# First adjacency chunks, first weight's queues, sum order and code rows of the second layer, last norm's order

## The chip, the cores and the metric

The kernel runs on one core of a Trainium2 chip. The metric is the device time of one execution in microseconds (us); the profile's span, from the first to the last instruction, is 1.8 us shorter.

## The reference, cut to what matters

Two graph layers on x (4096 x 512 float32) and adj (4096 x 4096 int32, about 32 ones in a row).

```python
# layer 0: at most the first 64 neighbours of a row
keep = (adj > 0) & (cumsum(adj > 0, axis=1) <= 64)
cnt  = keep.sum(axis=1)
xj   = leaky_relu((keep @ x / max(cnt, 1)) @ W_nb.T + b_nb)
xi   = leaky_relu(x @ W_line.T + b_line)
x1   = layernorm(x + xi + where(cnt > 0, xj, 0))
# layer 1: dense attention
wh   = x1 @ W + bW
e    = leaky_relu((wh @ a1 + b1)[:, None] + (wh @ a2 + b2)[None, :], 0.2)
out  = layernorm(x1 + softmax(where(adj > 0, e, -9e15)) @ wh)
```

## The kernel before

Rows are taken in 32 blocks of 128; "x i" below is block i of x, 256 KB, loaded by four DMAs of 64 KB. Five stages follow each other on TensorE (PE).

**Head (L362).** `load_squares` (L287) splits 128 rows of x, or a quarter of a weight, into four DMAs over a tuple of queues (SP, ACT, POOL); `turn_squares` transposes what has landed on VectorE (DVE). `by_quarters` multiplies x 0 with W_nb quarter by quarter, then x 1 with the whole of W_nb, then both with W_line. `spin` keeps PE busy until then. All DMAs of SP and ACT count their landings on eight semaphores in turn, those of POOL on eight others; each DMA waits, in its queue, for the earlier one on its semaphore. So at most eight of either kind are under way.

**y stage (`seven`, L493).** Blocks go in pairs g = 1 to 15, and each pair takes seven products in this order: x_g with w11, x_p with t3 (p is the pair before), bank_z with t1, bank_w with w22, x_g with t2, x_p with t4, bank_y with w21. One step lasts 12.04 us on PE. `turn_pair` (L294) transposes the next two blocks on DVE and has POOL load two more (x tiles rotate over three buffers); L557 is the DVE sum that must have read x_p before the product with t4 writes there. Between the products, `steps` puts work in from lists of four: in steps 1 and 2 the DVE sums `fold_w(c)` (L379, folding W with a1 and a2), from step 3 on the codes of adj. A chunk of adj (1 MB, `load_adj`, L157, SP, two buffers) goes through `edge` on ScalarE (ACT, L168), scans on DVE and `pack`. `fold_end` writes the folded `wa` to DRAM (`wa_d`, L386, SP, 1024 single words).

**Aggregation (L738).** 32 blocks, 14.5 us each.

**wh stage (L1202, L889).** wh = x1 W. Steps j count 128 permuted rows; `seven_wh` takes a pair g in two parts. `turn_x1` (L821) transposes what `load_turned` (L795, SP) loaded; `first_wh` makes two quarter products, ACT copies one into `bt` (L898) and `sum_wh` (L901, DVE) adds the other into the bank `xv` on which the next products pile up. L939 is the ACT copy of `xv` into its neighbour half, for the product with t1. `sums_x1` (L878, L879) and `sums_x2` (L884, L885) are sums for the next pair. `load_nat` (L948) brings the first two halves of the code rows of block 0 on ACT's queue, four DMAs of 64 KB each; `cover` (L960) reads them first at step 7.

**Attention (L1075) and tail.** 64 parts of 56 products; after the last one the final two blocks are summed and normed on DVE (L1287 to L1290, `ln_rs`, `ln_apply`), with one power on POOL (L126) for each.

The order of instructions on each engine is written out by hand in these loops (`manual_schedule`), and each engine keeps it.

Of the kernel before, what the change touches and what calls it, by code (L numbers as in the profile page):

```python
# [8 lines left out]
F32 = mybir.dt.float32  # L9
# [10 lines left out]
P = 128  # L20
# [11 lines left out]
def two_layer_adj_gnn(  # L32
# [16 lines left out]
    nc = tc.nc  # L49
    N, C = x.shape  # L50
    NB = N // P
    NC = C // P
# [18 lines left out]
    stat = ctx.enter_context(tc.tile_pool(name="stat", bufs=4))  # L71
# [43 lines left out]
    def ln_stats(y):  # L115
        st = stat.tile([P, nc.vector.BN_STATS_DIM], F32, name="st")
        nc.vector.bn_stats(st, y)  # L117
        return ln_rs(st)
# [18 lines left out]
    with ExitStack() as l0:  # L137
# [12 lines left out]
        edge_of = {}  # L150
        seen_of = {}

        def load_adj(s):
            if s < NB * NCH:
                b, h = divmod(s, NCH)
                a = adj_p.tile([P, CH], I32, name="a")
                nc.sync.dma_start(a, adj_blk(b)[:, ts(h, CH)])  # L157
                loaded[s] = a

# [117 lines left out]
        with ExitStack() as la:  # L277
# [8 lines left out]

            def load_squares(dst, src, queues):  # L287
                for n in range(NC):
                    queues[n * len(queues) // NC].dma_start(  # L289
                        dst[ts(n, SQ)], src[:, ts(n, P)].rearrange("(j a) c -> a j c", a=SQ)  # L290
                    )

# [6 lines left out]
            def load_turned_x(i, queues=(nc.gpsimd,)):  # L299

                if i < NB:
                    xrs[i] = late[i % 3].rearrange("p (j c) -> p j c", c=P)
                    load_squares(xrs[i], x_blk(i), queues)
# [32 lines left out]
            def load_part(name, src, part, queues):  # L336
                load_squares(raw[name][:, part], src[P * part.start // NC : P * part.stop // NC, :], queues)

            def load_quarter(name, src, c, queues):
                load_part(name, src, slice(NC * c, NC * c + NC), queues)  # L340
# [35 lines left out]
            def fold_w(c):  # L376
                wn = raw["w"][c] if c < NC else early_rows[2]
                for k in range(2):
                    nc.vector.scalar_tensor_tensor(  # L379
                        early_rows[3], wn, 1.0, early_rows[k], ALU.mult, ALU.mult,  # L380
                        accum_out=wa[:, k, c : c + 1] if c < NC else ca[:, k : k + 1],
                    )
# [35 lines left out]
                    y_lo[i], src, y_hi[i].bitcast(F32), ALU.subtract  # L418
                )

            both = (nc.sync, nc.scalar)
            load_turned_x(0, both)
            load_quarter("nb", w_nb, 0, both)
            load_quarter("nb", w_nb, 1, (nc.gpsimd,))
            load_quarter("nb", w_nb, 2, (nc.sync,))
            load_quarter("nb", w_nb, 3, (nc.scalar,))
            load_turned_x(1, both)
            for h in range(2):
                load_part("line", w_line, slice(2 * NC * h, 2 * NC * (h + 1)), both)
            load_turned_x(2, both)  # L430
            spin(12)

            turn_x(0)
            load_turned_x(3, both)
            nc.sync.dma_start(bias_line, b_line.partition_broadcast(P))
            pys[0] = by_quarters(xts[0], "nb")
            turn_x(1)
            load_turned_x(4)
# [172 lines left out]
            for g in range(1, NT):  # L611
                steps = idle
                q = done[0]
                if g == 1:
                    steps = [
                        lambda: load_adj(0),
                        lambda: None,
                        lambda: nc.scalar.activation(few[:, 5:6], three, AF.Sigmoid),
                        lambda: fold_w(0),
                    ]  # L620
                elif g == 2:
                    steps = [
                        lambda: fold_w(1),
                        lambda: (load_adj(1), fold_w(2)),
                        lambda: None,
                        lambda: fold_w(3),
                    ]
                else:
                    flags = lambda: (load_adj(q + 2), edge(q + 1))
                    codes = (lambda: pack(q - 1)) if g > 3 else (  # L630
                        lambda: (edge(0), fold_w(NC), fold_end())
                    )

                    steps = [
                        flags if g > 4 else codes,
                        lambda: scan_sums(q),
                        codes if g > 4 else flags,
                        lambda: scan_codes(q),
                    ]
                    if g == NT - 1:  # L640
                        load_own_x(NB - 1, nc.gpsimd)
                        scan_first = steps[1]
                        steps[1] = lambda: (scan_first(), load_first_kt())
                    done[0] += 1
                seven(g, False, steps)
# [229 lines left out]
    def sums_x1(g):  # L875
        if PLAIN <= g < NS // 2:
            top, low = x1ts[2 * g], x1ts[2 * g + 1]
            nc.vector.tensor_tensor(sum_x(g, 1), low[:, 0:2], low[:, 2:4], ALU.add)  # L878
            nc.vector.tensor_tensor(low[:, 0:2], top[:, 0:2], low[:, 0:2], ALU.subtract)  # L879
# [20 lines left out]
    def sum_wh(g):  # L900
        nc.vector.tensor_tensor(xvs[g % 2][:, 0], bt[:, g, 2], yrs[g % 2][:, 1], ALU.add)  # L901

    def seven_wh(g, part, extra=lambda: None):

        p = g - 1
        new, old = g < NS // 2, p >= PLAIN
        yr, xv = yrs[g % 2], xvs[g % 2]
        yr_p, xv_p = yrs[p % 2], xvs[p % 2]  # L910
        t1, t2, t4, _ = wsums
        if part == 0:
            if new and g > PLAIN:
                first_wh(g)
            if old:
                product_wh(yr_p[:, 0], x1ts.pop(2 * p)[:, 2:4], w21)
                product_wh(xv_p[:, 1], sum_x(p, 1), t1)
            if g == PLAIN + 1:
                sum_wh(g)
            turn_x1(2 * g + 3)  # L920
            sums_x1(g + 1)
            if new and g > PLAIN + 1:
                sum_wh(g)
            if old:
                nc.scalar.copy(bt[:, p, 0:2], yr_p)
            extra()
        else:
            if old:
                product_wh(xv_p[:, 0], x1ts.pop(2 * p + 1)[:, 2:4], t4)
            if new:  # L930
                product_wh(xv[:, 0], sum_x(g, 2), t2)
                product_wh(yr[:, 1], sum_x(g, 4), w22)
            turn_x1(2 * g + 4)
            sums_x2(g + 1)
            if old:
                nc.scalar.copy(bt[:, p, 2:4], xv_p)
                later.append(p)
            if new:
                nc.scalar.copy(xv[:, 1], xv[:, 0])  # L939
            extra()  # L940

    def load_nat(b, h, queue=nc.sync):

        if b < NB:
            nats[b, h] = ep.tile([P, 2, NS * SQ // 2], BF16, name="nat")
            rows = code_d[b].rearrange("(i a) (n x) -> n a i x", a=SQ, n=4)
            for n in range(4):
                queue.dma_start(nats[b, h][ts(n, SQ)], rows[n][:, ts(h, 2), :])  # L948
# [242 lines left out]
    for j in range(NS):  # L1191
        g, h = divmod(j, 2)
        if g < PLAIN:
            if j == 3:

                first_wh(PLAIN)
                sum_wh(PLAIN)
            bank = ps_acc.tile([P, 2, HC], F32, name="acc")
            (yrs, xvs)[g].append(bank)
            x1t = x1ts.pop(j)  # L1200
            for m in range(NC):
                nc.tensor.matmul(  # L1202
                    bank.rearrange("p h c -> p (h c)"), x1t[:, m, :], ws[:, m, :],
                    start=(m == 0), stop=(m == NC - 1),
                )
            nc.scalar.copy(bt[:, g, 2 * h : 2 * h + 2], bank)
            if j == 2:
                sums_w1()
            turn_x1(j + 3)
            if j == 2:  # L1210
                sums_x1(PLAIN)
                sums_w2()
                sums_x2(PLAIN)
            if h == 1:
                later.append(g)
            if j == 3:
                sums_w3()
        else:
            seven_wh(g, h, lambda: weights_step(j))
        load_turned(j + 7)  # L1220
        if j in (1, 2):
            load_nat(0, j - 1, nc.scalar)
        if j in (5, 7):
            combine_wh()
    seven_wh(NS // 2, 0)
# [59 lines left out]
    nc.vector.bn_stats(st[:, 1], low[:, 1])  # L1285
    for h in range(2):
        stt(top[:, h], p[2 + h], rz[:, 0:1], top[:, h], ALU.mult, ALU.add)  # L1287
    top_stats = ln_stats(top.rearrange("p h c -> p (h c)"))
    stt(low[:, 0], p[4], less_rz, low[:, 0], ALU.mult, ALU.add)
    nc.vector.bn_stats(st[:, 0], low[:, 0])  # L1290
    low_stats = ln_rs(st)
    ln_apply(top.rearrange("p h c -> p (h c)"), top_stats)
# [38 lines left out]
```

## Time and profile before

| what | us |
|---|---|
| three runs | 1552.64, 1552.98, 1554.51 (median 1552.98) |
| the profiled execution | 1552.42, its span 1550.6 |
| PE busy | 1538.0 (99%) |
| DVE, ACT, POOL busy | 1267.5, 984.2, 263.1 |
| PE before the first product (L362) | 6.36, with idle products from 1.21 |
| y stage starts, aggregation starts | 21.8, 204.09 |
| wh stage starts, attention starts | 668.44, 769.59 |
| record of the attention's last product ends | 1543.29 |

A line of the timeline has start, duration, engine, source line, operation, out<-in, shapes and, in brackets, how long the engine stood idle before and what released it. The windows have the busy time of each engine in each stretch, the granted clock, the mean busy share of the 16 DMA engines (DMA) and GB/s. A float32 product is two records on PE. Records of one run overlap, since their ends are modelled; so the pace is read from the distance of their starts (0.43 us for 128x512, 0.216 us for 128x256).

### The profile page before, as it was taken

The numbers are of one execution on the slowest core, as the hardware profiler recorded it, in microseconds if no ns is written. First come the engines' busy times: TensorE is split into PE (matmuls) and PEld (weight loads), VectorE is DVE, ScalarE is ACT, GpSimd is POOL, SyncE is SP. The second block draws the span as 40 slices with busy tenths as digits, with TensorE's granted clock in tenths as the row PEclk, the third lists the DMA queues.
The fourth block names the chain that finished last, engine by engine and source line by source line (L and its number), as shares of the span: only waits on it lengthen the run. The fifth ranks groups of instructions, "written<-read, shape, count | busy, mean of one in ns | idle before, by whom it ended". The sixth has DMA issues, their size and how long they took to land.

```text
span 1550.6 us, 19180 instructions
## 1 busy us (share of the span) xinstructions
PE 1538.0 (99%) x6580; PEld 1240.4 (80%) x6580; DVE 1267.5 (82%) x2348; ACT 984.2 (63%) x1186; POOL 263.1 (17%) x422
## 2 busy tenths in 40 slices
PE   9999999999999999999999999999999999999998
PEld 5444478888888888868888888888888888888887
DVE  6888769999999999378887888888888888888864
ACT  2666678888888887427684567555675556755520
POOL 4545322212221212110001101111011110111101
PEclk9999999999999999999999999999999999999999
DMA  9965598888998887654122112221122211222202
GB/s 238 206 207 185 193 254 263 226 269 264 250 260 256 234 263 189 153 126 113 42 61 56 46 36 69 63 60 48 35 69 64 59 49 34 69 66 57 51 5 55
DMA packets 180098, 203.28 MB, mean 131 GB/s; under 512 B 102416, under 2 KB 141072, under 8 KB 171680
## 3 DMA queue, kind: packets, MB, share of 16 engines
q1 hardware_dynamic: 149424, 131.25, 29.5%
q0 software_dynamic: 26416, 68.43, 17.4%
q10 hardware_dynamic: 4160, 2.38, 0.6%
q8 instruction: 51, 0.84, 0.2%
q14 instruction: 47, 0.39, 0.1%
HBM read 142.08 MB, written 43.13 MB: 119 GB/s over the span
## 4 chain that ended last, share of the span: by engine, by line
PE 96%; DMA 2%; DVE 1%; issue 0%; ACT 0%; POOL 0%; SPq 0%; ACTq 0%; DVEq 0%; POOLq 0%
PE acc L1075 36%; PE acc L738 28%; PE pt L1075 14%; PE acc L493 11%; PE acc L889 4%; PE pt L738 2%; PE acc L362 1%; DMA c<-in_x_dram 1%; DMA nat<-code_d 0%; DMA w<-x_d 0%; DMA a<-in_L_gnn_W_nb_dram 0%; DVE c L821 0%; DVE a L821 0%; POOL c L289 0%; DVE st L117 0%
## 5 line engine op out<-in xcount | busy, mean ns | idle before, releaser
L1075 PE MATMUL acc<-bt,s 128*128 128x256 f32 x1504 | 335.7, 379 | 0.0
L1075 PEld LDWEIGHTS acc<-bt,s 128*128 128x128 f32 x1504 | 285.8, 190 | 38.9
L738 PE MATMUL acc<-y_hi,kt 128*128 128x512 f32 x780 | 303.4, 389 | 0.0
L738 PE MATMUL acc<-y_lo,kt 128*128 128x512 f32 x780 | 303.4, 389 | 0.0
L960 ACT ACTIVATE w<-nat,few 128x1024 f32<-128x1024 uint8 x128 | 137.0, 1137 | 237.4 <-DVE a L1035 237.4
L1075 PE MATMUL acc<-bt,a 128*128 128x256 f32 x1056 | 239.0, 379 | 0.0
L1075 PE MATMUL pt<-bt,a 128*128 128x256 f32 x992 | 224.5, 379 | 0.0
L1075 PEld LDWEIGHTS acc<-bt,a 128*128 128x128 f32 x1056 | 200.6, 190 | 27.3
L1075 PEld LDWEIGHTS pt<-bt,a 128*128 128x128 f32 x992 | 188.5, 190 | 25.6
L1035 DVE STREAM_TRANSPOSE a<-w 128x1024 f32<-128x1024 f32 x128 | 153.1, 1225 | 61.8 <-ACT w L1016 51.0
L271 ACT ACTIVATE kt<-ktb,few 128x1024 fp32r<-128x1024 uint8 x124 | 142.6, 1151 | 86.5 <-PE acc L738 68.9
L126 POOL TENSOR_TENSOR rs<-ve,few 128x1 f32<-128x1 f32 x64 | 42.7, 666 | 810.3 <-DVE ve L124 797.0
L738 PEld LDWEIGHTS acc<-y_hi,kt 128*128 128x128 f32 x780 | 146.5, 188 | 30.4
L738 PEld LDWEIGHTS acc<-y_lo,kt 128*128 128x128 f32 x780 | 146.5, 188 | 30.3
L953 ACT ACTIVATE w<-w,st_n 128x1024 f32<-128x1024 f32 x128 | 149.3, 1233 | 16.4 <-DVE m L970 16.4
L1016 ACT ACTIVATE w<-w,nm 128x1024 f32<-128x1024 f32 x128 | 145.5, 1137 | 11.1 <-DVE nm L1007 11.1
L970 DVE CUSTOM_DVE_ANT_0 w<-e_n,w 128x1024 f32<-128x1024 f32 x128 | 149.5, 1220 | 1.3
L168 ACT ACTIVATE edge<-a,few 128x2048 bf16<-128x2048 int32 x64 | 136.3, 2129 | 1.8 <-DVE left L187 1.7
L216 ACT CAST code<-left 128x2048 uint8<-128x2048 bf16 x64 | 121.1, 1893 | 0.0
L199 DVE TENSOR_TENSOR left<-edge,left 128x2048 bf16<-128x2048 bf16 x64 | 78.4, 1225 | 2.2
L187 DVE TENSOR_TENSOR_SCAN left<-few,ends,left 128x1024 bf16<-128x1024 f32 x32 | 75.2, 2351 | 1.1
L187 DVE TENSOR_TENSOR_SCAN left<-few,left 128x1024 bf16<-128x1024 f32 x32 | 73.3, 2291 | 1.1
(230 smaller groups left out, 2041.9 us busy)
## 6 DMA issues: line engine op xcount, KB each, us to landing
a<-in_adj_dram SPq DMA_DIRECT2D x64, 1024.0 KB, 5.8
code_d<-code POOLq DMA_DIRECT2D x64, 256.0 KB, 3.9
nat<-code_d SPq DMA_DIRECT2D x248, 64.0 KB, 2.2
w<-x_d SPq DMA_DIRECT2D x128, 64.0 KB, 2.1
own<-in_x_dram SPq DMA_DIRECT2D x31, 256.0 KB, 3.1
own<-own_d POOLq DMA_DIRECT2D x31, 256.0 KB, 5.1
x_d<-own POOLq DMA_DIRECT2D x31, 256.0 KB, 4.8
out_dram<-c POOLq DMA_DIRECT2D x30, 256.0 KB, 2.7
```

Of the source, the lines that this page charges most:

```text
L168: nc.scalar.activation(edge_of[s], loaded.pop(s).rearrange("p (t q) -> p q t", q=2), AF.Sigmoid, bias=steep[:, 0:1], scale=STEEP, accum_ou ...
L187: nc.vector.tensor_tensor_scan(left[:, 1], three.to_broadcast([P, CH // 2]), left[:, 0], NEIGHBORS + 3.0 if h == 0 else end, ALU.max, ALU. ...
L216: nc.scalar.copy(code.bitcast(U8).rearrange("p (t q) -> p q t", q=2), seen_of.pop(s))
L271: nc.scalar.activation(kts[s], bytes_.rearrange("p t (i r) -> p t r i", r=2), AF.Sigmoid, bias=steep[:, 1:2], scale=STEEP,)
L493: nc.tensor.matmul(bank, lhs[:, k, :], rhs[:, k, :], start=start and k == 0, stop=k == 1, skip_group_check=True,)
L738: nc.tensor.matmul(accs[i], kt[:, k // 2, k % 2, :], term[j], start=(g == n == 0 and term is y_hi), stop=(g == NS - 1 and n == KB - 1 and ...
L953: nc.scalar.activation(dst, src, AF.Prelu, bias=bias, scale=scale, alpha=0.2)
L960: nc.scalar.activation(wts[b][:, i, :], nats[b, i // 2].bitcast(U8)[:, i % 2, :], AF.Relu, bias=far, scale=-FAR,)
L970: nc.vector.tensor_tensor_reduce(w_i, e2_n, w_i, 1.0, -3e38, ALU.subtract, ALU.max, m4s[b][:, i : i + 1])
L1016: nc.scalar.activation(w_i, w_i, AF.Exp, bias=nms[b][:, i : i + 1], accum_out=z4s[g][:, r, i : i + 1])
L1035: nc.vector.transpose(a[:, r].rearrange("p s (i a) -> p i s a", a=SQ), wts[2 * g + r][:, :, ts(k, 8 * SQ)].rearrange("p i (s x) -> p i s x ...
L1075: nc.tensor.matmul(banks[g][n], lhs[:, j, :], bt[:, 4 * k + j, rhs, :], start=(k == 0 and j == 0 and n == mate[0]), stop=(k == NP - 1 and ...
```

## The change

1. **Adj chunks 0 and 1** are no longer asked for in steps 1 and 2 as they are; each load now follows a one-column memset on DVE that stands behind `fold_w(1)` and `fold_w(3)`, and so waits for them.
2. **Head:** `load_squares` deals its four DMAs out in turn. The quarters of W_nb go over SP, ACT and POOL (5, 5 and 6 DMAs, before 6, 6 and 4), x 1, x 2 and x 3 partly over POOL, and b_line is asked for before x 2 and x 3.
3. **wh stage:** `sum_wh` stands ahead of `sums_x1` on DVE. The eight DMAs of the first code rows are issued after step 3 instead of after steps 1 and 2; in ACT's order they now stand between the copy of step 3 (L1206) and the first copy L939.
4. **Tail:** the sum of the lower block's first half stands ahead of the upper block's aggregation (L122) and the wait for its power.

The products on PE keep their order and number; DVE has two memsets more.

```diff
-        def load_adj(s):
+        def load_adj(s, behind=None):
...
                 a = adj_p.tile([P, CH], I32, name="a")
+                if behind is not None:
+                    behind.memset(a[:, 0:1].bitcast(F32), 0.0)
                 nc.sync.dma_start(a, adj_blk(b)[:, ts(h, CH)])
...
-                    queues[n * len(queues) // NC].dma_start(
+                    queues[n % len(queues)].dma_start(
...
-            both = (nc.sync, nc.scalar)
-            load_turned_x(0, both)
-            load_quarter("nb", w_nb, 0, both)
-            load_quarter("nb", w_nb, 1, (nc.gpsimd,))
-            load_quarter("nb", w_nb, 2, (nc.sync,))
-            load_quarter("nb", w_nb, 3, (nc.scalar,))
-            load_turned_x(1, both)
+            sp, act, pool = nc.sync, nc.scalar, nc.gpsimd
+            load_turned_x(0, (sp, act))
+            load_quarter("nb", w_nb, 0, (sp, act, pool, pool))
+            load_quarter("nb", w_nb, 1, (sp, act, pool, pool))
+            load_quarter("nb", w_nb, 2, (sp, act, pool, sp))
+            load_quarter("nb", w_nb, 3, (act, sp, pool, act))
+            load_turned_x(1, (sp, act, pool, pool))
             for h in range(2):
-                load_part("line", w_line, slice(2 * NC * h, 2 * NC * (h + 1)), both)
-            load_turned_x(2, both)
+                load_part("line", w_line, slice(2 * NC * h, 2 * NC * (h + 1)), (sp, act))
+            nc.sync.dma_start(bias_line, b_line.partition_broadcast(P))
+            load_turned_x(2, (act, pool))
             spin(12)
 
             turn_x(0)
-            load_turned_x(3, both)
-            nc.sync.dma_start(bias_line, b_line.partition_broadcast(P))
+            load_turned_x(3, (sp, pool))
...
                 if g == 1:
                     steps = [
-                        lambda: load_adj(0),
+                        lambda: None,
                         lambda: None,
...
                 elif g == 2:
                     steps = [
-                        lambda: fold_w(1),
-                        lambda: (load_adj(1), fold_w(2)),
+                        lambda: (fold_w(1), load_adj(0, nc.vector)),
+                        lambda: fold_w(2),
                         lambda: None,
-                        lambda: fold_w(3),
+                        lambda: (fold_w(3), load_adj(1, nc.vector)),
                     ]
...
             turn_x1(2 * g + 3)
-            sums_x1(g + 1)
             if new and g > PLAIN + 1:
                 sum_wh(g)
+            sums_x1(g + 1)
...
-        if j in (1, 2):
-            load_nat(0, j - 1, nc.scalar)
+        if j in (3, 4):
+            load_nat(0, j - 3, nc.scalar)
...
-    top_stats = ln_stats(top.rearrange("p h c -> p (h c)"))
+    top_st = stat.tile([P, nc.vector.BN_STATS_DIM], F32, name="st")
+    nc.vector.bn_stats(top_st, top.rearrange("p h c -> p (h c)"))
     stt(low[:, 0], p[4], less_rz, low[:, 0], ALU.mult, ALU.add)
+    top_stats = ln_rs(top_st)
     nc.vector.bn_stats(st[:, 0], low[:, 0])
```

## Prediction

> **What bounds the kernel now.** The page first, whose two lines say what there is to win:
>
> ```profile
> PE 1538.0 (99%) x6580; PEld 1240.4 (80%) x6580; DVE 1267.5 (82%) x2348; ACT 984.2 (63%) x1186; POOL 263.1 (17%) x422
> PE 96%; DMA 2%; DVE 1%; issue 0%; ACT 0%; POOL 0%; SPq 0%; ACTq 0%; DVEq 0%; POOLq 0%
> ```
>
> PE is busy but for 12.6 us of the 1550.6, and the change takes no product away. So a gain can only come from PE's holes and from the tail. Where PE waits says the view of its waits (us in total, times, longest):
>
> ```profile
> PE acc L493 <- DVE t L557: 1.6, 1, 1.6
> PE acc L889 <- DVE acc L901: 1.6, 2, 1.1
> PE acc L362 <- DVE wt_nb L294: 0.8, 1, 0.8
> ```
>
> Each of the three is touched by one part. Idle times understate them, as a record's end is modelled; I measure from start to start. The y stage, chain of waits first, then PE's timeline:
>
> ```profile
> 28.12 1.65 POOL c L289 x3
> 29.77 7.78 DMA c<-in_x_dram
> 38.31 0.66 DVE t L557
> ```
> ```profile
> 35.54 1.88 PE L493 MATMUL acc<-hi,lo 128*128 128x512 f32 x4
> 39.01 1.98 PE L493 MATMUL acc<-hi,xt 128*128 128x512 f32 x4 [1.59 <-DVE t L557]
> 40.84 3.60 PE L493 MATMUL acc<-wt_nb,xt 128*128 128x512 f32 x8
> ```
>
> The fourth DMA of x 7 takes 7.78 us from issue to landing; DVE waits for it (3.34 us), then L557, then PE. From 35.54 to 40.84 are 5.30 us for two products that elsewhere take 1.715 each: the hole costs 1.87. Meanwhile SP has both adj chunks under way, issued at 24.0 and 25.4. The windows show the head and a spot to be wary of (columns as in the table's note):
>
> ```profile
> 7.00:8.00 1.00, 0.96 (x9) 0.77 (x7) 0.51 (x1) 0.00 (x0) 0.00 (x0) 1.00 0.55 123
> 8.00:9.00 1.00, 0.72 (x7) 0.53 (x5) 0.29 (x1) 0.00 (x0) 0.00 (x0) 1.00 0.61 179
> 46.00:47.00 1.00, 1.00 (x4) 0.52 (x3) 0.93 (x5) 1.00 (x1) 1.00 (x3) 1.00 0.00 0
> ```
>
> From 7 to 9 the DMA engines are 0.55 and 0.61 busy while PE waits for W_nb: too little is under way, since SP and ACT may not issue. At 46 nothing moves at all, though x 11 has been asked for at 45.83: `wa_d`, issued at 43.74, takes 12.7 us to land (DMA issues), and x 11's four DMAs need 11.2 to 12.1. Last the wh stage, timeline of ACT, DVE and PE:
>
> ```profile
> 680.37 2.23 ACTq L948 DMA_DIRECT2D nat<-code_d  x4
> 685.21 0.36 ACT L939 COPY acc<-acc 128x256 f32<-128x256 f32 x1 [0.33 <-PE acc L889]
> 687.98 0.71 DVE L821 STREAM_TRANSPOSE a<-w 128x512 f32<-128x512 f32 x1 [2.05 <-DMA w<-x_d]
> 690.96 0.42 DVE L901 TENSOR_TENSOR acc<-bt,acc 128x256 f32<-128x256 f32 x1
> ```
> ```profile
> 691.44 1.13 PE L889 MATMUL acc<-s,bt 128*128 128x256 f32 x4 [1.14 <-DVE acc L901]
> 697.83 1.13 PE L889 MATMUL acc<-s,bt 128*128 128x256 f32 x4
> 704.56 1.13 PE L889 MATMUL acc<-s,bt 128*128 128x256 f32 x4 [0.42 <-DVE acc L901]
> ```
>
> DVE gets x1's rows of step 8 2.05 us late, because code rows, x1 rows and broadcasts share the DMA engines; L901 stands behind that, and PE behind L901. By starts, less 0.865 for four records and counting the 0.105 of a restart, the three holes cost 1.42, 0.35 and 0.68.
>
> **Part by part. Head.** No DMA more or less. Quarter 0 now waits for POOL's second DMA; POOL's first four took 2.9 to 3.6 us to land, so it lands near 5.6 instead of 5.4. Quarter 1 (product at 7.56) needs POOL's fourth, as before, so that costs nothing. Quarters 2 and 3 land in turn instead of together, and POOL adds DMAs while SP and ACT wait. If they come just in time, PE goes on from 7.56: four quarters, x 1 next at 10.25 and W_line at 13.7 instead of 14.80, that is 1.1 less. If DMA is the limit after all, 0. I take 1.0, nearer the upper end, as the engines stood 0.84 us idle in those two windows. x 1 comes over three queues as well, so W_line, b_line, x 2 and x 3 are asked for about 1 us sooner. Of POOL's row, what follows is x 4; it is moved past four DMAs at about 0.55 us each, but waits for the transpose of x 1 anyway. The Trainium skill's page "DMA: Bandwidth & Descriptors", section "Issuing engines are not separate DMA queues", speaks against this part: all queues end in the same 16 engines, and spreading saves only issue time. By it this term would be near 0 and the whole 1.0 us smaller; the two windows with idle engines are why I do not follow it here.
>
> **Chunks.** Without 2 MB of adj, what is left in front of x 7 is W, a1, a2 and bW, which also start earlier. x 7 has to land by about 34 instead of 37.55, and its first DMA goes at 28.12 or sooner; even the 5.1 us that POOL's loads of x take at the median is then in time. The hole of 1.87 goes; if something is left of it, at most half. DVE pays two memsets (0.06 each, as that at 10.91), hidden, since DVE stood 3.34 us here. Chunk 0 now leaves at about 33, after `fold_w(1)`; with the 5.8 us of the median chunk, doubled, it lands by 45, and ACT's `edge(0)` (45.49 before, 42.6 after the shift) has some 3 us by the median. Chunk 1 leaves behind `fold_w(3)`, which without DVE's wait ends at about 39.7; `edge(1)` wants it at 47.2. Behind it in SP's queue stands `wa_d`, which so far went with an empty queue. What is late next: x 11, blocked by `wa_d` until 58.96. From its landing to the end of L557 are 1.41 us, and PE's next t4 product, at 63.15 before, comes at 60.3. So x 11 must land by 58.9: no slack is left, each us later costs PE one. Chunk 1 landing at 45.5 puts `wa_d` where it was (its small packets run at 44.5 to 45.7 before), and x 11, asked for at 42.5 to 44 now, may pass ahead. I take 0 for it, with 0 to 2 for the range.
>
> **wh stage.** `sum_wh` moved past two sums of 0.34 to 0.46 pitch is 0.8 earlier; the holes of 0.35 and 0.68 need 0.35 and 0.68. They go: 1.0 us. The two sums are read a pair later. With no code rows at 678 to 688 (8 x 64 KB), x1's rows of step 8 come in time and the 1.42 goes as well. But ACT issues eight DMAs behind the copy at 684.29, and L939 (685.21), L898, L925 and every later copy queue behind them. The first four go at 0.45 each, until 685.7; the next four wait for the landings of the first. PE wants L939's result at 688.41. With landings of 2.0 us the last goes at 687.7, L939 ends at 688.4 and PE loses 0; with the 5.9 of the slowest row it ends at 692.3 and PE loses 3.9; with the median of 2.9, 0.9. DMA is at 0.88 to 1.16 from 680 to 689, lighter by half a MB then; I take 3.6, so a loss of 1.4 against the 1.42 won: 0 (from +1.4 to -2.5).
>
> **Tail.** The sum (L1289) starts when the last product is done, near 1543.3, instead of at 1543.53; aggregation and addition follow it, and the lower statistics start at about 1544.05 instead of 1544.04. Nothing, within 0.15 to either side.
>
> **Sum.** 1.0 + 1.87 + 1.0 + 0 + 0 = 3.9 us off the profiled execution: span 1546.7, time 1548.5. The median of the runs lies 0.56 above that execution, so 1549.1. About 0.2% (3.1 us) is what a measurement of this kernel can tell from no change.
>
> **Rivals.** (1) ACT's queue blocks: PE loses 2.5 us more than I took, and gains stay at 1.4 to 2.5: 1550.5 to 1551.6. For it: ACT issued the last four in 2.23 us, at the landings' pace. Against: step 3 is past the worst of the broadcasts. Chance 0.18. (2) The head does not do what it says, DMA being the limit: 2.9 us, 1550.1. For it, 0.9 busy from 2 to 7 us. Chance 0.12. (3) Slower: chunk 1 lands as slowly as chunks did here (11.7 to 15.4 us), `wa_d` goes behind it and closes the DMA engines for its 12.7 us until 64 to 67 instead of 57; x 11 and chunk 2 stand behind. x 11 at 67 costs PE 8, net 4 slower: 1557. It decides from 62.8 on, 3.9 past 58.9; up to there it only eats the gain. Against it: those chunks ran two at a time beside W, and a late `wa_d` lets x 11 pass. Chance 0.08, and 0.05 for half of it (1551). The forecast itself, all parts about as summed: 0.57.
>
> **Numbers.** The forecast holds 1547.5 to 1549.8, from a head of 1.1 and ACT's block of 0 to a chunk term of 1.5. Of it and some of rival 2 come 0.62 for faster; rivals 1, 2 and half of 3 give 0.30 for the same; 0.08 slower. The range, 1547.5 to 1552.0, reaches over rivals 1, 2 and the half of 3.
>
> **What would show it.** Right: second quarter pair at about 8.5 and W_line's product at 13.7; no PE wait on L557; aggregation at 201.2; L939 of step 5 ending near 689.7 relative to the old clock, and no PE wait on L901. Wrong: the pairs start at 9.5 as before; x 11 landing after 59 with PE waiting on L557 near 60; a PE wait on L939 of over 2 us; the attention starting less than 2 us earlier than at 769.59.

## The result and the profile after

The changed kernel takes 1556.27 us (median of 21 runs, 1553.79 to 1557.91), the kernel before 1553.58 beside it (21 runs, 1551.87 to 1554.90): ratio 1.0018, 95% interval 1.0011 to 1.0025. So it is 2.7 us slower, where the forecast was 1549.1, that is 3.9 faster. The profiled execution took 1556.24, span 1554.5, at its median; the profiled one of before, 1552.42, lay 1.2 under the median of these 21, so the two traces differ by 3.9 us of span where the medians differ by 2.7. Two executions behind the tables below lie far off all others and are left out of the ratios: one of the kernel before (8155.08 us) and the profiled one of a2_no_head (3282.49 us).

The page says that PE is as busy as before. The waits of PE (us in total, times, longest) say that two of the three old ones are gone, that the one for W_nb has grown from 0.8 to 2.0 us, and that a new one, for ACT's copy L941, is longer than any of them:

```profile
PE 1538.9 (99%) x6580; PEld 1241.0 (80%) x6580; DVE 1267.1 (82%) x2350; ACT 983.8 (63%) x1186; POOL 271.0 (17%) x430
```
```profile
PE acc L891 <- ACT acc L941: 3.3, 1, 3.3
PE acc L364 <- DVE wt_nb L296: 2.0, 3, 1.4
...
PE acc L364 <- DVE wt_line L296: 0.5, 1, 0.5
PE acc L495 <- ACT acc L551: 0.5, 1, 0.5
```

(Lines of the changed kernel stand 2 further down: L941 is the L939 of before, L559 its L557, L950 its L948.) Since PE has the same 6580 matmuls in the same order, the two traces can be laid side by side product by product. How late the changed kernel is, at the same product:

| product (its start before) | late by, us |
|---|---|
| first product (6.36) | 0.55 |
| y stage starts (21.81) | 1.35 |
| fourth product of the y stage (26.96) | 2.24 |
| after the hole at L557 (40.84) | 0.38 |
| wh stage, last one before the new wait (687.54) | 0.22 |
| wh stage, after it (688.41) | 3.73 |
| 693.27 | 4.11 |
| 704.56, and from there on | 3.2 |
| last landing of the output | 3.2 |

From the last landing to the end of the span are 2.3 us before and 2.9 after: a closing drain on POOL's queue, which the timeline does not list, takes 5.48 us instead of 4.83 and ends 0.6 later after that landing. The table has the result in three readings. **The head lost 2.2 us** (PE's timeline, first before, then the changed kernel):

```profile
6.36 2.36 PE L362 MATMUL acc<-wt_nb,xt 128*128 128x128 f32 x16
9.48 5.49 PE L362 MATMUL acc<-wt_nb,xt 128*128 128x128 f32 x24 [0.76 <-DVE wt_nb L294]
14.80 7.17 PE L362 MATMUL acc<-wt_line,xt 128*128 128x128 f32 x40
21.81 1.88 PE L493 MATMUL acc<-wt_nb,xt 128*128 128x512 f32 x4
```
```profile
6.91 1.16 PE L364 MATMUL acc<-wt_nb,xt 128*128 128x128 f32 x8 [1.42 <-DVE wt_nb L296]
8.32 2.05 PE L364 MATMUL acc<-wt_nb,xt 128*128 128x128 f32 x16 [0.25 <-DVE wt_nb L296]
10.70 4.76 PE L364 MATMUL acc<-wt_nb,xt 128*128 128x128 f32 x16 [0.33 <-DVE wt_nb L296]
...
17.84 5.49 PE L364 MATMUL acc<-wt_line,xt 128*128 128x128 f32 x24 [0.53 <-DVE wt_line L296]
23.16 1.88 PE L495 MATMUL acc<-wt_nb,xt 128*128 128x512 f32 x4
```

The quarters no longer come two at a time, but the first starts at 6.91 (before 6.36), the second at 8.32 (7.56) and the fourth at 10.70 (10.36); only the third is 0.17 earlier. The last of W_nb landed at 9.74 (before 8.77), the last of W_line at 16.88 (14.99), the last of x 2 and x 3 at 20.32 (18.21). Of the 2.2 us the last 0.9 come in the y stage, before the fourth product, where PE waits for ACT's copy L551 (last line of the waits, 0.5 by the idle time). **The hole before L557's reader is closed**, as forecast; from 37.78 the products follow at 1.72 (same view):

```profile
37.78 1.88 PE L495 MATMUL acc<-hi,lo 128*128 128x512 f32 x4
39.50 1.88 PE L495 MATMUL acc<-hi,xt 128*128 128x512 f32 x4
41.21 3.60 PE L495 MATMUL acc<-wt_nb,xt 128*128 128x512 f32 x8
```

**The wh stage lost 3** (timeline of ACT and PE):

```profile
684.52 7.12 ACTq L950 DMA_DIRECT2D nat<-code_d  x8
...
691.73 0.36 ACT L941 COPY acc<-acc 128x256 f32<-128x256 f32 x1 [6.63 <-DMA nat<-code_d]
...
692.14 1.13 PE L891 MATMUL acc<-s,bt 128*128 128x256 f32 x4 [3.35 <-ACT acc L941]
...
693.11 1.47 PE L891 MATMUL acc<-s,c 128*128 128x256 f32 x4
...
694.37 1.91 PE L891 MATMUL acc<-s,bt 128*128 128x256 f32 x4
...
696.07 1.47 PE L891 MATMUL acc<-w,bt 128*128 128x256 f32 x4
```

The eight issues occupy ACT's queue for 7.12 us: the first four go out by 685.85, and each of the last four waits until one of these has landed, which takes them 4.7 to 5.4 us. The copy behind them starts at 691.73 instead of 685.21, and PE stands 3.35 us. Four matmuls of 128x256 take 0.87 us elsewhere; here the groups at 693.11 and 694.37 take 1.26 and 1.70 from start to start. The windows say why (busy time and count of PE, PEld, DVE, ACT, POOL, then the granted clock, DMA share, GB/s):

```profile
694.00:697.00 3.00, 3.00 (x9) 2.37 (x8) 2.90 (x8) 1.21 (x3) 0.00 (x0) 0.51 0.49 136
697.00:702.00 5.00, 5.00 (x25) 4.41 (x24) 3.22 (x9) 1.85 (x4) 0.00 (x0) 1.00 0.42 118
```

After the wait the granted clock fell to a half for 3.41 us, from 693.55 to 696.97: eight matmuls in 3.39 us instead of 1.73, another 1.7 us lost.

### The profile page after: what moved, and what is told of

It reads as the page before. It is cut to its first block, busy times and chain, and to the rows that moved or that the text cites. A ratio compares the mean times of both kernels' runs of the same rounds, so it can differ in the third digit from the quotient of the medians.

```text
span 1554.5 us, 19179 instructions
## 1 busy us (share of the span) xinstructions
PE 1538.9 (99%) x6580; PEld 1241.0 (80%) x6580; DVE 1267.1 (82%) x2350; ACT 983.8 (63%) x1186; POOL 271.0 (17%) x430
## 4 chain that ended last, share of the span: by engine, by line
PE 97%; DMA 2%; DVE 0%; ACT 0%; issue 0%; ACTq 0%; POOLq 0%; DVEq 0%
PE acc L1077 36%; PE acc L740 28%; PE pt L1077 14%; PE acc L495 11%; PE acc L891 5%; PE pt L740 2%; PE acc L1204 1%; DMA a<-in_L_gnn_W_nb_dram 1%; DMA nat<-code_d 0%; DMA a<-in_L_gnn_W_line_dram 0%; DMA c<-in_x_dram 0%; DVE t L397 0%; DVE hi L502 0%; DVE hi L516 0%; ACTq L291 0%
## 5 line engine op out<-in xcount | busy, mean ns | idle before, releaser
L126 POOL TENSOR_TENSOR rs<-ve,few 128x1 f32<-128x1 f32 x64 | 46.7, 730 | 814.1 <-DVE ve L124 794.1
L1018 ACT ACTIVATE w<-w,nm 128x1024 f32<-128x1024 f32 x128 | 145.5, 1138 | 11.1 <-DVE nm L1009 11.0
L495 PE MATMUL acc<-hi,lo 128*128 128x512 f32 x160 | 73.9, 593 | 0.5 <-ACT acc L551 0.5
```

Of the source, the lines that this page charges most:

```text
L495: nc.tensor.matmul(bank, lhs[:, k, :], rhs[:, k, :], start=start and k == 0, stop=k == 1, skip_group_check=True,)
L1018: nc.scalar.activation(w_i, w_i, AF.Exp, bias=nms[b][:, i : i + 1], accum_out=z4s[g][:, r, i : i + 1])
```

## The experiments

Two theories after these readings. **Theory 1:** the moved code rows cost what ACT's queue and then the clock take, and the head costs some 2 us, but only once the chunk part has closed the hole that would hide it. **Theory 2** (rival): the parts add up as measured alone, and the difference is their order or the extra traffic. All times are medians; "against before" is the ratio to the runs of before that were taken beside the kernels of a table (1553.91 in the first table, 1553.87 in the second, 1555.13 in the third).

### One part alone

The four edits are those of the diff above, one in each kernel.

**h1_head** (the diff's `load_squares` and head lines):

> The first-weight part alone (the order and queues of the first loads), everything else as before. Theory 1, the spread order makes the DMA engines slower for the same rows: the y stage starts at 23.2 instead of 21.8 and its third step is 2.2 us late, as in the changed kernel; what of that reaches the end depends on the hole before L557's reader (it ended at 40.84 before): +0.4 if that end is set by rows that land no later, +2.2 if it moves along. Theory 2, as the prediction had it: the second and third quarter come just in time, y stage at 20.8, -1.0 us at the end. Theory 3: only the position of x's rows changed, the stage starts within 0.2 us of 21.8, 0 at the end.

**c1_chunks** (its `load_adj` and `steps` lines):

> The chunk part alone (the first two chunks of adj issued behind the folds). Theory 1, the hole of 1.6 us before the reader of L557 goes and nothing new stands in its place: -1.8 us at the start of the aggregation stage and at the end. Rival, the chunk loads now block the engines that carry the later x rows: the hole is gone but a new wait of 1 to 6 us stands between 45 and 70 us, 0 or slower at the end.

**s1_sums** (the two lines below):

```diff
-            sums_x1(g + 1)
             if new and g > PLAIN + 1:
                 sum_wh(g)
+            sums_x1(g + 1)
```

> The two lines of seven_wh alone: sum_wh ahead of sums_x1. Theory 1, as in the prediction: the holes of 0.35 and 0.68 us before the sum's reader vanish and the hole of 1.42 us at 691.44 (rows late) stays: -1.0 us at the end. Rival: sums_x1 comes later by one sum (0.43 us) and its readers wait as long: 0 at the end.

**n1_nat:**

```diff
-        if j in (1, 2):
-            load_nat(0, j - 1, nc.scalar)
+        if j in (3, 4):
+            load_nat(0, j - 3, nc.scalar)
```

> The move of the first codes' rows alone (from steps 1 and 2 to steps 3 and 4 on ACT's queue). Theory 1, the eight issues stand in ACT's queue ahead of the copy at L939 and each waits for a DMA lane that SP's row loads hold: the copy that started at 685.21 starts near 691.7, PE waits 3.3 us for it, and the 1.42 us hole at 691.44 is gone: +2.5 us at the end (between +2.0 and +3.8). Rival, the loss in the changed kernel comes from the order of the sums together with the move: within 0.5 us of no change here.

| kernel | us | against before, interval | in us |
|---|---|---|---|
| h1_head | 1552.66 | 0.9995 (0.9987 to 1.0004) | -1.3 |
| c1_chunks | 1550.72 | 0.9979 (0.9970 to 0.9988) | -3.2 |
| s1_sums | 1552.79 | 0.9993 (0.9984 to 1.0002) | -1.1 |
| n1_nat | 1556.26 | 1.0015 (1.0006 to 1.0024) | +2.4 |

The chunk part gains more than its hole of 1.87, the sums about what their two holes are worth, the move costs; the head alone can't be told from no change, although its y stage starts 1.58 us late in its trace: the hole at L557 is then gone (0.57 late behind it), for x 7 lands at 37.91 (before 37.55) and PE comes for it that much later. The four differences add up to -3.2, and together with the tail the parts gave +2.7. So they don't add up, and theory 2 is in trouble already.

Laid beside before product by product, these traces also differ where nothing was edited. The hole at 691.44 is shorter by 1.31 us in h1_head's, 1.07 in c1_chunks's and 0.95 in s1_sums's, though the code rows stand where they stood. It is mostly this hole that takes h1_head's trace from 0.27 us late to 1.29 early. So a part alone, set against before, has the changes of that hole in its number.

The move alone shows the same block as in the changed kernel, with a shorter wait (timeline of n1_nat):

```profile
687.66 6.38 ACTq L948 DMA_DIRECT2D nat<-code_d  x8
...
694.13 0.36 ACT L939 COPY acc<-acc 128x256 f32<-128x256 f32 x1 [5.89 <-DMA nat<-code_d]
...
694.54 1.13 PE L889 MATMUL acc<-s,bt 128*128 128x256 f32 x4 [2.61 <-ACT acc L939]
```

After these 2.61 us the clock stayed at 1.00 and the matmuls at 0.216 apart. PE is 3.36 us late ahead of this wait and 3.84 at the start of the attention, so by this trace the move costs 0.5 net; what it costs with the half-rate stretch is read from the changed kernel's trace and from b1 and a2 below. The 3.36 come from elsewhere: the same execution had a longer hole at L557 than before's, though nothing there was edited, and that one did cost the clock (PE's timeline, then the windows):

```profile
40.64 3.11 PE L493 MATMUL acc<-hi,xt 128*128 128x512 f32 x4 [3.15 <-DVE t L557]
```
```profile
40.00:44.00 4.00, 3.36 (x5) 1.50 (x6) 3.93 (x12) 1.34 (x3) 3.28 (x7) 0.67 0.39 121
```

So before's hole is not 1.6 us in every run: 1.59 and 1.64 (s1_sums) in two traces, 3.15 and a half-rate stretch in a third. That bears on c1_chunks, which gained 3.2 where one trace promised 1.87. It is not the only candidate: in c1_chunks's own trace the hole at L557 gives 1.86 and the one at 691.44 the 1.07 named above. The mean granted clock of the runs fits the first, without proving it: of 32 runs of before beside it 12 had 0.999 and took 1552.9 on average, 18 had 0.998 and took 1554.5, 2 had 0.997 (1554.4); all 11 of c1_chunks had 0.999. But this mean also counts the time after the last product, which b2_nat_pool's trace shows at half clock, and b2_nat_pool's runs at 0.998 and at 0.999 differ by 0.06 us.

### Parts taken out of the changed kernel, and parts put together

**a1_no_nat** (changed kernel with `load_nat` back at steps 1 and 2):

> The changed kernel with the first codes' rows back at steps 1 and 2. Theory 1, the parts overlap: the reordered head delays the y stage by some 2.2 us and only the chunk part's removed hole pays for it, so that the stage of wh is entered 0 to +0.5 us against before, and the sums' order takes 1.0 there (2.2 if the hole at 691.44 goes too, as it did with the head alone): -0.5 to -2.2 us against before. Rival, the parts add up as measured alone (-1.2, -3.2, -1.1): -5.5 us. Either way 3 to 5 us below the changed kernel, if the move is what costs.

**a2_no_head** (changed kernel with the first loads of before):

> The changed kernel with the first loads as before. Theory 1, the reordered head costs about 2 us once the chunk part has taken away the hole that hid it: 1.5 to 2.5 us below the changed kernel, +0.3 to +1.2 against before. Rival, the head gives what it gave alone (-1.2) or nothing: at or above the changed kernel's time.

**b1_chunks_sums** (before with the chunk part and the sums' order):

> Before with the chunk part and the sums' order only. Theory 1: the chunk part's gain as measured alone (-3.2; by its trace -1.9) and the sums' holes (-1.0 by the trace): -2.9 to -4.2 us. Rival, with the chunk part the rows of x1's step 8 stand later against the products and the hole there grows by what the sums give: no better than the chunk part alone, -3.2.

**b2_nat_pool** (b1_chunks_sums, and):

```diff
-        if j in (1, 2):
-            load_nat(0, j - 1, nc.scalar)
+        if j in (3, 4):
+            load_nat(0, j - 3, nc.gpsimd)
```

> As the kernel with the chunk part and the sums' order, and the first codes' rows at steps 3 and 4 but issued by POOL instead of ACT. Theory 1, it was ACT's queue that made the move cost: the copy of step 5 starts within 0.3 us of its product, PE waits for it not at all, and the rest of the hole at 691 goes: 0 to -1.4 us against the kernel without the move. Rival, the transfers themselves are the cost (the rows of x1 land later by the 0.5 MB): a hole of 2 us or more stays at the same place, +2 us. Second rival, POOL's queue holds them behind the loads of e_n and st_n, and the first reader of the codes' rows waits on ACT near 693: +1 us or more.

| kernel | us | against before, interval | in us |
|---|---|---|---|
| a1_no_nat | 1551.81 | 0.9987 (0.9978 to 0.9996) | -2.1 |
| a2_no_head | 1553.42 | 0.9997 (0.9988 to 1.0006) | -0.5 |
| b1_chunks_sums | 1549.51 | 0.9971 (0.9961 to 0.9981) | -4.4 |
| b2_nat_pool | 1548.79 | 0.9968 (0.9957 to 0.9979) | -5.1 |

Theory 1 has a1 and b2 within its spans; b1 lies 0.2 below its span, and a2 0.8: without the head the changed kernel loses 3.2 us (from +2.7 to -0.5 against before) where 1.5 to 2.5 were expected. Theory 2 fails in all but b1, on which both agree. From b1 to a1 is the head (with the tail): +2.3. From b1 to a2 is the move on ACT: +3.9 (a2 has no trace that can be read, and it has the tail too). From a2 to b2 the same eight DMAs go out at the same steps, on POOL's queue instead of ACT's (and the tail goes): -4.6. It was the queue, not the transfers. Timeline of b2_nat_pool:

```profile
688.50 0.53 POOL L950 DMA_DIRECT2D nat<-code_d  x1 [0.18 <-issue]
...
689.43 0.36 ACT L941 COPY acc<-acc 128x256 f32<-128x256 f32 x1 [0.33 <-PE acc L891]
```

The last issue goes out at 688.50 past a copy that waits for nothing but PE, and no hole is left in the wh stage. This version beats both kernels.

### What the head costs, and which half of it

Base is b2_nat_pool, whose runs differ least (1548.63 to 1549.18). **e1_all** has the whole head part; **e2_w** only the quarters of W_nb over three queues; **e3_x** only the rows of x 1 to x 3 partly on POOL, and b_line earlier (in both W_line, in e2_w the rows of x too, are dealt out in turn over SP and ACT):

```diff
 e2_w
+            load_quarter("nb", w_nb, 0, (sp, act, pool, pool))
+            load_quarter("nb", w_nb, 1, (sp, act, pool, pool))
+            load_quarter("nb", w_nb, 2, (sp, act, pool, sp))
+            load_quarter("nb", w_nb, 3, (act, sp, pool, act))
 e3_x
+            load_turned_x(1, (sp, act, pool, pool))
...
+            nc.sync.dma_start(bias_line, b_line.partition_broadcast(P))
+            load_turned_x(2, (act, pool))
...
+            load_turned_x(3, (sp, pool))
```

**e4_tail** has the tail's order alone.

> The kernel with the chunk part, the sums' order and the codes' rows on POOL, plus the whole reordered head. Theory 1: the head costs what the runs with and without it differed by, +2.3 us against the same kernel without it (1548.8), so about 1551.1, with the y stage starting 1.5 us later than there. Rival: the 2.3 came from the state of the rows in the wh stage, which POOL's issue has now settled: 1549.3 or less.

> The same kernel without the head part, plus only the first weight's quarters spread over three queues; the rows of x stay on SP and ACT in their old places. Theory A, rows of x issued early by POOL displace the second weight: within 0.4 us of 1548.8 or below, second weight landed by 15.3. Theory B, with three queues at once each packet takes longer and the first weight lands later: about 1549.8, last quarter at 9.5 or later and the second weight as late.

> The same kernel without the head part, plus only the rows of x blocks 1 to 3 partly on POOL's queue and the bias earlier; the first weight's loads as before. Theory A (displacement): second weight landed near 16.5 instead of 15.0, y stage 1.2 to 1.5 us late, about 1550.5. Theory B (packets): first weight in time, about 1549.8.

> The same kernel without the head part, plus only the last norm's order. As the prediction had it: 0, within 0.15 us of 1548.8, time from the last product's start to the last landing 6.9 to 7.0 us as in both traces. Rival: the later start of the statistics of the lower half shifts its scale: +0.3.

| kernel | us | against before, interval | W_nb, W_line landed by |
|---|---|---|---|
| b2_nat_pool (from the second table) | 1548.79 | 0.9968 (0.9957 to 0.9979) | 8.7, 15.1 |
| e1_all | 1551.67 | 0.9980 (0.9972 to 0.9989) | 10.5, 17.0 |
| e2_w | 1549.99 | 0.9969 (0.9957 to 0.9981) | 9.8, 16.1 |
| e3_x | 1550.80 | 0.9979 (0.9969 to 0.9988) | 10.3, 15.8 |
| e4_tail | 1548.85 | 0.9964 (0.9952 to 0.9977) | 8.8, 15.0 |

The tail is nothing: 0.06 from base, within the spread of either. Against e4_tail, taken beside them, the whole head costs 2.8, its two halves 1.1 and 2.0. Part of this stands behind the last landing: from there to the end of the span, where POOL's drain is, are 2.6 us in b2_nat_pool and e4_tail, 2.7 in e2_w, 3.2 in e3_x and 3.4 in e1_all, so 0.8 of the whole head's cost; the traces do not say why it is longer. Of the two explanations packets (B) fit e2_w, and displacement (A) fits e3_x, though there W_nb was displaced more than W_line. The DMA queues from 4 to 9 us, first in b2_nat_pool, then e2_w, then e3_x (packets, MB, share of the 16 engines' time):

```profile
q1 hardware_dynamic: 991, 0.45, 33.6%
q10 hardware_dynamic: 931, 0.42, 33.3%
q0 software_dynamic: 99, 0.19, 13.9%
```
```profile
q10 hardware_dynamic: 730, 0.33, 38.2%
q1 hardware_dynamic: 763, 0.34, 35.6%
q0 software_dynamic: 159, 0.32, 31.3%
```
```profile
q0 software_dynamic: 259, 0.54, 44.2%
q1 hardware_dynamic: 802, 0.37, 31.2%
q10 hardware_dynamic: 715, 0.33, 27.7%
```

With W_nb spread, POOL's queue (q0) moves more and SP's and ACT's (q1, q10) less, and each of their packets takes longer: 0.356 x 16 x 5 us / 763 = 37 ns on q1 instead of 27, 42 instead of 29 on q10. In the five traces with W_nb spread they take 37 to 44 ns, in the seven with its loads and those of x as before 27 to 33. The sum is 0.99 MB instead of 1.06, which says little, for the kernel before moves 1.00 in the same 5 us. With the rows of x on POOL and W_nb as before (e3_x) the sum is larger, 1.24 MB, and the packets take 31 ns, though POOL's share is largest there. But 0.54 MB is POOL's, most of that rows of x, which it issues from 3.74 us on, and W_nb's last quarter lands at 10.3 instead of 8.7: they get in ahead. (The profiled execution of e2_w was its slowest, 1551.92; the landings of W_nb in e1_all, h1_head, a1_no_nat and the changed kernel, all with the spread, agree with it: the last by 9.7 to 10.5.) Why SP's and ACT's packets take longer when POOL carries part of W_nb is not shown.

## Why the prediction was wrong, point by point

**Head, -1.0 forecast: this step failed, in sign too.** It measured +2.8 (e1_all) or +2.3 (b1 to a1). The reason was the windows at 7 and 8 us with the DMA engines 0.55 and 0.61 busy, read as time in which a third queue would bring W_nb sooner. It did not: the same rows over three queues landed about 1 us later (W_nb by 9.7 to 10.5 in five traces, by 8.7 to 9.2 in the seven with the loads of before), and quarters 0 and 1, which were to start at no cost, started 0.5 and 0.8 us late in the changed kernel. That more can be moved is so (1.24 MB in e3_x), but what moved were other rows. The Trainium skill's page "DMA: Bandwidth & Descriptors", section "Issuing engines are not separate DMA queues", was weighed and set aside; it would have brought the term to 0, nearer than -1.0, and the measurement goes beyond it: the part cost time. The second error was in "W_line, b_line, x 2 and x 3 are asked for about 1 us sooner", counted as harmless: POOL asked for its halves of x 2 and x 3 from 5.87 us on, ahead of W_line (from 7.17), and they landed at 11.1 to 13.6, W_line's last at 16.88. The second rival had the first half of this, with 0 for its price, not a loss.

**Code rows, 0 forecast: this step failed by size.** The mechanism was the one described, eight issues ahead of the copy L939, and the hole of 1.42 did go, as most of it did in h1_head and c1_chunks without the move. The block was priced by a landing of 3.6 us, 1.4 for PE. The four landings that the last four issues waited for took 4.7 to 5.4 us, and the block measured 3.35 in the trace, close to the far end of the bounds (3.9): ACT's queue held 7.12 us for eight issues. And a term was missing: the 1.7 us of half clock after it. The sum of the traces, 3.35 - 1.42 + 1.7 = +3.6, or 3.9 from start to start (0.22 late before the wait, 4.11 at 693.27), is what b1 to a2 measured (+3.9); the range ended at 2.5. The first rival named this block with 1550.5 to 1551.6 and stopped there for the same missing term.

The Trainium skill's page "TensorE: Matmul & The Clock Gate", section "Part 1: The HAM clock gate", says that the clock is halved after an idle window of about 3.4 us and comes back after as long a busy one. The traces agree on the length of the half-rate stretch: 3.41 us in the changed kernel (from 693.55), in n1_nat (from 41.36) and in s1_sums (from 7.81, in the head). They do not agree that PE must stand as long: the waits ahead were 3.35, 3.15 and 1.82 us, and in the 3.41 us just before the half-rate stretch PE stood 2.0, 2.7 and 1.8 of them. In each trace the granted clock changes only at whole multiples of 3.41 us after its first change. Counted in such pieces, n1_nat's wait of 2.61, which was not followed by half rate, lies on both sides of a border, 1.31 and 1.30 us; before's hole of 1.59 lies within one piece, and the most that passed without half rate before the last product is 1.71 (e2_w, from 23.2). So here it is the share of one piece that counts, with the limit between 1.71 and 1.82 us, not the length of the wait; these are 13 traces, and no run was made to test it.

**Chunks, -1.87 forecast: right mechanism, size short.** Measured -3.2 (-4.7 to -1.9). In c1_chunks's trace the hole gives the 1.86 forecast, and 1.07 more come from the hole at 691.44. In some runs of before the hole at L557 may also be longer, with the clock behind it, as n1_nat's trace shows once; how the extra 1.3 us divide is open. The worry behind it did not come true: in the changed kernel chunk 1 landed at 50.69, `wa_d` at 58.87 and x 11 at 59.77, 0.9 later than the bound of 58.9, and PE, 0.4 late itself, did not wait; the bound was too strict by half a microsecond or more. So the third rival, slower by way of `wa_d`, is refuted, though its sign came true by other causes.

**Sums, -1.0: right.** -1.2 on top of the chunk part (c1 to b1); the two holes of 0.35 and 0.68 are gone from b2_nat_pool's trace, and 0.8 of their 1.03 us from s1_sums's. That s1_sums gave -1.1 alone may be in part luck: its trace has 0.95 less at 691.44 as well, and a head 1.42 late. **Tail, 0: right,** 0.06. From the start of the last product to the last landing are 6.96 us before, 6.98 after.

**The sum.** Head 2.3 to 2.8, chunks -3.2, sums -1.2, code rows +3.9: +1.8 to +2.3, against 2.7 measured. Of the signs of failure that the prediction listed, the wait on L941 of over 2 us and the late attention (+3.2 instead of earlier) are there; the third quarter still starts near 9.5, at 9.31, and the fourth at 10.70.

## What to carry to other kernels

A DMA issue is an instruction of its engine's queue: where it has to wait for a semaphore, as four of the eight did here, it shuts that engine until an earlier DMA has landed (7.12 us in all), so such issues belong on the queue whose next work is wanted last. Idle DMA engines beside a waiting PE do not show that another queue brings the awaited rows sooner; price such a part with no gain at best, and check what gets in ahead of the rows that are wanted first. And price a new wait of PE of 2 us or more with the half-rate stretch that may follow: here 3.35 us of waiting brought 1.7 more.

## What the runs showed that was not expected

- A wait of PE of 3.35 us cost 1.7 us more at half clock (694 to 697, clock 0.51), one of 2.61 nothing, and one of 1.82 was followed by half clock again: the length of the wait alone does not decide. The hole at L557, where nothing was edited there, measured 1.6 us in two traces and 3.15 in a third; before, which has it, spreads over 3 us and more each time it was measured with 20 runs or more; b2_nat_pool, which has none, over 0.55 in its six runs. That the hole makes the scatter is likely, not shown.
- SP's and ACT's packets slowed down when POOL took a larger part of W_nb: 27 to 29 ns became 37 to 42 as POOL's share rose from 14% to 31%. The share alone does not do it, for at 44% with rows of x instead (e3_x) they took 31.
- The kernel's end got longer with the loads moved to POOL: from the last landing to the end of the span are 2.3 us before, 2.6 with the code rows on POOL, 2.9 with the head, 3.4 with both.
- A part that costs 2.8 us in a kernel without holes (e1_all) cost nothing measurable in one with a hole 15 us further on (h1_head): that hole took up all but 0.57 us of the delay, and the hole at 691.44, shorter by 1.31 in its trace, the rest.
